# Layer 0 of a four-layer network: reciprocals of the norms spread by DMA, zeroing issued by SyncE, other mask shares, a third copy buffer, the image in eight pieces

## The chip, the cores and the metric

The kernel runs on one core of a Trainium2 chip. The metric is device time in microseconds (us): the median of several runs. One execution was also taken with the hardware profiler. Its *span* is the time from the first to the last recorded instruction; what lies around the span belongs to the run's time but not to the profile.

## What is computed

The reference is a network of four layers on one image of 256 channels and 64x64 positions. Only layer 0 is touched by the change:

```
x  = x + layer0(group_norm(x))                 # layers 1 to 3 follow
q, k = sigmoid(Wq x), sigmoid(Wk x);  v = Wv x, then divided by its norm per head and position
for w in (1, 2, 4):                            # windows of 64, 32 and 16 positions a side
    wk   = box sum of k over the window;   wkv = box sum of k v^T over the window
    attn = q . wkv ;   norm = q . wk           # per head (8 heads of 32 channels) and position
    out_w = attn / (norm + 1e-6)
layer0 = Wout [out_1, out_2, out_4] + bout
```

There is no softmax: the attention is linear, with a window as mask. Later layers contain two mixtures of experts. Their token lists `xs` (8 times 4096 rows of 256 numbers in DRAM) must be zero before rows are scattered into them; that zeroing is issued from inside layer 0.

## The kernel before, in words

**Tiles.** The 4096 positions are cut into 8 blocks of 512 (`I`, eight image rows each), and each block into 4 tiles of 128 (`J`, 8x16 positions). The 8 heads are done in two halves (`hf`) of four heads, since four heads of 32 channels fill 128 partitions. A tile name begins with `l_` in the profile where the code says `l0_`.

**Start.** `run` loads the image into `xc` with two DMAs of 2 MB, one issued by SyncE (SP) and one by ScalarE (ACT). `layer0` makes a selection matrix `sel` on GpSimd (POOL), then the window masks (`masks0`: small VectorE (DVE) operations make rows and columns, POOL multiplies them out), then `group_norm`: 16 `bn_stats` on DVE (L157) and the normalised image `y` (L162). `project0` computes q, k, v; `norms0` computes the three norms of all positions with box sums on DVE, POOL and ACT, collects them in PSUM with matmuls (L401) and takes reciprocals into `rec` (L403, L404), one row for each combination of window, block and head: 96 rows of 512.

**Main stage.** Then the pools of that stage are closed and those of the next opened: `l0o` (output weights, a zero tile), `l0w` (work) and PSUM. `half0` runs per half. POOL first builds running sums of the k v^T states of whole tiles (`F32_`, `R`, `F64_`: L415 to L424) and copies them into block-diagonal matrices `bd` (`states`, L431) when they are needed. Work then goes in *regions* (`region0`), each a list of *jobs*:

- for each half and each half image `ih`: four regions `J` for the window of 64, whose result is kept in `far["o"]`; then, for each block `I`, a region of 4 jobs that completes the window of 64 (part 0) and a region of up to 20 jobs for the windows of 32 and 16 (part 1).
- A job has a *first* part: scores of one key tile against up to four query tiles, four matmuls into the PSUM tiles `s` (L511), one tile for each pair of heads. The scores are multiplied by masks into `sm` (L529). Pair 0 is always masked by DVE, straight from PSUM. Pair 1 is first copied to SBUF by ACT (`sc`, L520, two buffers) and then masked by POOL or DVE.
- Its *second* part multiplies `sm` by v and adds into PSUM accumulators a, b, c (L553). It comes two jobs later (`self.second`).

POOL or DVE for pair 1 is decided at build time: two running sums `load0` estimate the load of both engines, with a price per mask and per tile of it, and POOL takes the mask when its sum would stay below.

**Order.** PE's (TensorE's) instructions are in the order written (`manual_schedule`). All other engines are ordered by a planner: it simulates the program with its own costs and lets each engine take the earliest written instruction that is ready. An instruction that comes late in the code but waits for nothing can thus be placed early. Each engine, SP included, then runs its list strictly in order. A tile pool has `bufs` copies per tag; a new tile waits until the last user of the old one is done.

**Output.** Results of a block go into a list `self.later`, and one entry is done after each job's first part (`out_rows`, L566). For each of three windows, `scale` spreads `rec` over the 32 channels of each head with a matmul `sel x rec` into the PSUM tile `x` and multiplies on DVE (L581). `project` then multiplies by the output weights (L137, tile `l_x_ps`, out of `l_o` and `w_out`) and adds to the image rows `xs`, which are loaded (L592) and stored to `xd` (L607) by SP.

**Zeroing.** `clear_list` is called once for each block of half 0 and has ACT issue a DMA of 4 MB that copies the zero tile over one eighth of the token lists (L1512).

Of the kernel before, what the change touches and what calls it, by code (L numbers as in the profile page):

```python
# [10 lines left out]
F32 = mybir.dt.float32  # L11
# [8 lines left out]
P = 128  # L20
# [59 lines left out]
class Net:  # L80
# [183 lines left out]
    def layer0(self, xc, x, xd, done):  # L264

        nc, tc = self.nc, self.tc
        mom = self.mom
        with tc.tile_pool(name="l0", bufs=1) as pool:
            q = [pool.tile([P, N], F32, tag=f"q{hf}", name=f"l0_q{hf}") for hf in range(2)]
            k = [pool.tile([P, N], F32, tag=f"k{hf}", name=f"l0_k{hf}") for hf in range(2)]  # L270
            v = [pool.tile([P, NT, P], F32, tag=f"v{hf}", name=f"l0_v{hf}") for hf in range(2)]
            S = [pool.tile([P, NT, D], F32, tag=f"S{hf}", name=f"l0_S{hf}") for hf in range(2)]
            rec = [pool.tile([3 * D, NB], F32, tag=f"rec{hf}", name=f"l0_rec{hf}") for hf in range(2)]
            sel = pool.tile([3 * D, NBLK, 4, D], F32, tag="sel", name="l0_sel")
            for wi in range(3):
                qs = slice(wi * D, (wi + 1) * D)
                nc.gpsimd.tensor_copy(sel[qs], bc(self.ident[qs, qs].rearrange("p (a b) -> p a b", b=4), 3, D))
            with tc.tile_pool(name="l0m", bufs=1) as tmp:
                M = self.masks0(pool, tmp)
            with tc.tile_pool(name="l0y", bufs=1) as ypool:  # L280
                self.consts0(ypool)
                y = ypool.tile([P, 2, N], F32, tag="y", name="l0_y")
                tiled = lambda a: a.rearrange("p (i j r c) -> p i r j c", i=NBLK, j=4, r=TR)
                raster = lambda a: a.rearrange("p (i r j c) -> p i r j c", i=NBLK, r=TR, j=4)
                self.group_norm(xc, lambda m: [(tiled(y[:, m])[:, i], raster(xc[:, m])[:, i]) for i in range(NBLK)])
                done()
                with (
                    tc.tile_pool(name="l0g", bufs=1) as gpool,
                    tc.tile_pool(name="l0a", bufs=2) as wp,
                    tc.tile_pool(name="l0a_ps", bufs=2, space=PSUM) as ps,  # L290
                ):
                    self.weights(ypool, ["w_qk0", "w_kv0"])
                    for hf in range(2):
                        self.project0(hf, y, q[hf], k[hf], v[hf], S[hf], wp, ps)
                        self.norms0(q[hf], k[hf], rec[hf], gpool, wp, ps)
            with (
                tc.tile_pool(name="l0o", bufs=1) as wop,
                tc.tile_pool(name="l0w", bufs=2) as wp,
                tc.tile_pool(name="l0_ps", bufs=1, space=PSUM) as ps,
            ):  # L300
                self.weights(wop, ["w_out0"])
                self.zero = wop.tile([P, C], F32, tag="zero", name="zero")
                nc.gpsimd.memset(self.zero, 0.0)
                self.load0 = [0.0, 0.0]
                bd = [[wp.tile([P, 4, P], F32, tag=f"bd{wi}{i}", name=f"l0_bd{wi}", bufs=1) for i in range(2)] for wi in range(2)]
                for b in bd[0] + bd[1]:
                    nc.gpsimd.memset(b, 0.0)
                st = [pool.tile([P, NBLK, 6], F32, tag=f"st{m}", name="l0_st") for m in range(2)]
                self.later, self.second = [], []
                with tc.manual_schedule(engines={mybir.EngineType.PE}):  # L310
                    for hf in range(2):
                        self.half0(hf, q[hf], k[hf], v[hf], S[hf], rec[hf], sel, M, bd, x, xd, st, wp, ps)
                    for go in self.second:
                        go()
                    while self.later:
                        self.later.pop(0)()
                for m in range(2):
                    nc.vector.bn_aggr(mom[:, m, :], st[m])
# [37 lines left out]

    def norms0(self, q, k, rec, ypool, wp, ps):

# [16 lines left out]
        for i in range(NBLK):  # L375
            for wi, ws in enumerate(WINS):
# [17 lines left out]
                if b > a:  # L394
# [6 lines left out]
                nc.tensor.matmul(p[wi * D : (wi + 1) * D, :], self.head_at[:, i, :], pr.rearrange("p j r c -> p (j r c)"),  # L401
                                 start=(i == 0), stop=(i == NBLK - 1))
        nc.vector.tensor_scalar_add(rec, p[: 3 * D], 1e-6)  # L403
        nc.vector.reciprocal(rec, rec)  # L404

    def half0(self, hf, q, k, v, S, rec, sel, M, bd, x, xd, st, wp, ps):
        nc, w = self.nc, self.w
        I8 = lambda a: a.rearrange("p (i j) e -> p i j e", j=4)

        F32_ = wp.tile([P, NT, D], F32, tag="F32", name="l0_F32", bufs=1)  # L410
        R = wp.tile([P, NT, D], F32, tag="R", name="l0_R", bufs=1)
        F64_ = S
# [22 lines left out]
        for ih in range(2):  # L435
# [10 lines left out]

            def rows_of(I, part, far=far, ih=ih):
                return lambda accs: self.out_rows(hf, I, accs, far["o"][:, I - 4 * ih, :], rec, sel, x, xd, st, wp, ps, part)

# [12 lines left out]
            for I in range(4 * ih, 4 * ih + 4):  # L462
                if hf == 0:
                    self.clear_list(I)

                jobs = []
                di = 4 if I < 4 else -4
# [5 lines left out]
                self.region0({"a": []}, jobs, k, v, wp, ps, rows_of(I, 0))  # L473

                b = states(1, F32_, I, slice(4 * I, 4 * I + 4))
                jobs = []
                for di in (-2, 2, -1, 0, 1):
                    if not 0 <= I + di < NBLK:
                        continue
                    for Jk in range(4):  # L480
                        j0, j1 = max(0, Jk - 1), min(3, Jk + 1)
# [12 lines left out]
    def region0(self, full, jobs, k, v, wp, ps, after):  # L494
# [12 lines left out]
        def first(i):  # L507
# [4 lines left out]
            ns = [len(range(*o[1].indices(n))) for o in outs]  # L512
            dve = sum(0.06 + 0.27 * t for t in ns)
            pool = sum(0.07 + 0.43 * t for t in ns)
            sms = []
            for pair in range(2):
                src, eng = s[pair], nc.vector
                if pair == 1:
                    src = wp.tile([P, 2, n, P], F32, tag="sc", name="l0_sc")
                    nc.scalar.copy(src, s[pair])  # L520
# [46 lines left out]

    def out_rows(self, hf, I, accs, o64, rec, sel, x, xd, st, wp, ps, part):

# [5 lines left out]

        def scale(wi, acc):
            def go():
                p = ps.tile([P, NB], F32, tag="x", name="l0_x_ps")
                ws = slice(wi * D, (wi + 1) * D)
                self.mm(p, [(sel[ws, I].rearrange("p h f -> p (h f)"), rec[ws, :])])  # L580
                nc.vector.tensor_mul(o[:, wi, :], o[:, wi, :], p)  # L581
            return go

        if part == 0:
            self.later.append(scale(0, None))
            return
# [10 lines left out]
        def project(m):  # L597
# [10 lines left out]
            return go  # L608
        self.later += [scale(1, None), scale(2, None), project(0), project(1)]

# [897 lines left out]

    def clear_list(self, k):

        part = self.xs[k * N : (k + 1) * N, :].rearrange("(p a) c -> p a c", p=P)
        self.nc.scalar.dma_start(out=part, in_=bc(self.zero, 1, N // P))  # L1512

# [410 lines left out]
    def run(self, x, out):  # L1924
        tc, nc = self.tc, self.nc
        with tc.tile_pool(name="const", bufs=1) as cpool, ExitStack() as left:
# [3 lines left out]
            for m in range(2):  # L1930
                (nc.sync, nc.scalar)[m].dma_start(out=xc[:, m, :], in_=x[m * P : (m + 1) * P, :])
            self.constants(cpool)
# [151 lines left out]
```

## Time and profile before

| | |
|---|---|
| median of 17 runs | 4570.07 us (4557.12 to 4582.64) |
| the profiled execution: its own time | 4571.75 us |
| its span | 4570.0 us |
| granted TensorE clock over the span | 0.91 |
| image, masks, group norm | 0 to 35 us |
| projections and norms of both halves | 35 to 313 us |
| main stage, half 0 | 313 to about 987 us |
| main stage, half 1 | about 987 to 1529 us |
| layers 1 to 3 | from 1530 us |
| busy over the span: PE, DVE, ACT, POOL | 83%, 40%, 26%, 33% |
| zeroing DMAs: 8 of 4096 KB | 28.3 us median from issue to landing |

How to read it: the page divides the span into 40 slices of 114 us and gives the busy share of each engine in tenths. Groups of instructions are listed by line, engine and operation, with the busy time, the mean length of one in ns, and the time that the engine sat idle just before them with the engine that ended the wait. A matmul of 32-bit numbers appears as two instructions. DMA-issuing instructions stand in the timeline with a queue's name (`SPq`, `ACTq`); their length is how long they held the engine that issues them.

### The profile page before, as it was taken

Reading aid. Unit: us, or ns where it says so; the run is one execution under the profiler, and the core shown is the slowest. Engines: PE = TensorE matmul, PEld = TensorE weight load, DVE = VectorE, ACT = ScalarE, POOL = GpSimd, SP = SyncE. Lnnn points to the kernel's source line nnn. Section 1 sums busy time; section 2 is a strip of 40 time slices with the busy share of each in tenths; the row PEclk is TensorE's granted clock in tenths of the full one; section 3 lists DMA queues with packets and bytes.
Section 4 is the critical chain, followed back from the end, with each engine's and each line's share of the span. In section 5 each row is a group of like instructions: output and inputs, shape, how many; then the busy total and the mean of one; then the engine's idle time right before and its main releaser. Section 6 shows DMA issues by size and latency. Waiting matters only on the chain.

```text
span 4570.0 us, 56172 instructions
## 1 busy us (share of the span) xinstructions
PE 3781.0 (83%) x22396; PEld 2384.7 (52%) x22396; DVE 1836.1 (40%) x3350; ACT 1180.5 (26%) x1979; POOL 1508.4 (33%) x1409
## 2 busy tenths in 40 slices
PE   6756999799999667666658877899999999799993
PEld 3311333333333356654446655566666666688882
DVE  5763565456666445545656632601111100100003
ACT  3322233233333154332112211222222212222220
POOL 3683666766666133433334300400000000000005
PEclk9867999899999888887878789999999999899996
DMA  1026000000000411110000176200000000455553
GB/s 47 0 92 214 20 19 2 19 20 10 20 10 20 141 44 56 51 44 27 0 0 29 46 225 199 64 0 10 10 10 10 10 10 10 184 194 194 194 182 118
DMA packets 149279, 291.72 MB, mean 64 GB/s; under 512 B 15248, under 2 KB 94480, under 8 KB 138768
## 3 DMA queue, kind: packets, MB, share of 16 engines
q1 hardware_dynamic: 95520, 210.01, 13.9%
q10 hardware_dynamic: 41200, 44.46, 2.9%
q0 software_dynamic: 12288, 33.57, 2.3%
q8 instruction: 178, 2.92, 0.3%
q14 instruction: 93, 0.76, 0.1%
HBM read 199.89 MB, written 88.10 MB: 63 GB/s over the span
## 4 chain that ended last, share of the span: by engine, by line
PE 43%; DVE 4%; DMA 2%; issue 2%; ACT 1%; POOL 1%; SPq 0%; POOLq 0%; DVEq 0%; ACTq 0%
PE a_o_ps L1830 10%; PE a_s_ps L137 10%; PE f_h_ps L137 8%; PE f_y_ps L137 7%; PE a_qkv_ps L137 2%; DMA f_g<-ys,f_back 1%; PE a_q_ps L137 1%; PE f_x_ps L1681 1%; DVE a_sm L1277 1%; PE a_o_ps L137 1%; PE a_u_ps L137 1%; PE a_c_ps L1302 1%; PE f_r_ps L137 0%; PE tr_ps L200 0%; DMA f_w<-in_f_w 0%
## 5 line engine op out<-in xcount | busy, mean ns | idle before, releaser
L529 POOL TENSOR_TENSOR l_sm<-l_sc,mask 128x768 f32<-128x768 f32 (+3 forms) x473 | 658.8, 1412 | 407.0 <-ACT l_sc L520 350.8
L529 DVE TENSOR_TENSOR l_sm<-l_s,mask 128x512 f32<-128x512 f32 (+3 forms) x624 | 486.5, 803 | 441.8 <-PE l_s L511 439.1
L511 PE MATMUL l_s<-l_q,l_k 32*128 32x384 f32 (+2 forms) x3584 | 493.8, 530 | 110.1 <-ACT l_sc L520 57.8
L520 ACT COPY l_sc<-l_s 128x512 f32<-128x512 f32 (+3 forms) x448 | 339.4, 758 | 841.2 <-PE l_s L511 680.3
L1830 PE MATMUL a_o_ps<-a_v,a_e 128*128 128x257 f32 x2048 | 484.3, 380 | 0.0
L137 PE MATMUL a_s_ps<-a_qT,a_kT 128*128 128x512 f32 x1024 | 482.4, 593 | 0.0
L1830 PEld LDWEIGHTS a_o_ps<-a_v,a_e 128*128 128x128 f32 x2048 | 389.1, 190 | 160.1 <-issue 118.6
L511 PEld LDWEIGHTS l_s<-l_q,l_k 32*128 32x128 f32 x3584 | 182.4, 187 | 427.4 <-DVE l_sm L529 224.1
L1724 POOL DMA_INDIRECT f_g<-ys,f_back x128 | 123.2, 962 | 811.8 <-DMA ys<-f_y 571.4
L137 PE MATMUL f_h_ps<-f_xT,f_w 128*128 128x256 f32 x1560 | 368.1, 387 | 19.0 <-ACT f_h L1693 13.4
L1593 POOL DMA_INDIRECT xs<-f_n,f_to x64 | 61.6, 963 | 921.6 <-DVE f_to L1590 643.2
L137 PE MATMUL f_y_ps<-f_w,f_h 128*128 128x256 f32 x1560 | 363.0, 380 | 2.5
L137 PEld LDWEIGHTS f_h_ps<-f_xT,f_w 128*128 128x128 f32 x1560 | 284.9, 191 | 91.1 <-ACT f_h L1693 32.5
L1825 ACT ACTIVATE a_e<-a_s_ps 128x512 f32<-128x512 f32 x256 | 152.9, 597 | 694.0 <-PE a_s_ps L137 694.0
L1693 ACT ACTIVATE f_h<-f_h_ps,f_w 128x256 f32<-128x256 f32 x390 | 184.9, 474 | 543.5 <-PE f_h_ps L137 536.9
L137 PEld LDWEIGHTS f_y_ps<-f_w,f_h 128*128 128x128 f32 x1560 | 289.0, 190 | 45.6 <-ACT f_h L1693 10.2
L818 PE MATMUL l_acc_ps<-ident,l_pr 128*128 128x128 f32 x1600 | 208.2, 290 | 121.0 <-DVE l_pr L814 116.9
L137 PEld LDWEIGHTS a_s_ps<-a_qT,a_kT 128*128 128x128 f32 x1024 | 192.3, 190 | 141.7 <-issue 129.6
L818 PEld LDWEIGHTS l_acc_ps<-ident,l_pr 128*128 128x128 f32 x1600 | 193.0, 151 | 135.9 <-DVE l_pr L814 129.2
L814 DVE TENSOR_TENSOR l_pr<-l_vk,l_w_ps 128x1280 f32<-128x1280 f32 x128 | 182.3, 1480 | 96.7 <-ACT l_w_ps L803 86.1
L1683 DVE COPY f_xT<-f_x_ps 128x512 f32<-128x512 f32 x78 | 53.9, 692 | 385.8 <-PE f_x_ps L1681 385.8
L553 PE MATMUL l_b_ps<-l_sm,l_v 128*32 128x256 f32 (+2 forms) x2176 | 176.3, 383 | 27.7 <-POOL l_sm L529 27.7
(411 smaller groups left out, 4742.8 us busy)
## 6 DMA issues: line engine op xcount, KB each, us to landing
f_w<-in_f_w SPq DMA_DIRECT2D x39, 1152.0 KB, 5.6
f_w<-in_f_w SPq DMA_DIRECT2D x39, 1028.0 KB, 7.2
xs<-zero ACTq DMA_DIRECT2D x8, 4096.0 KB, 28.3
l_vk<-vt SPq DMA_DIRECT2D x180, 128.0 KB, 2.9
f_x<-xs SPq DMA_DIRECT2D x78, 256.0 KB, 5.4
ys<-f_y SPq DMA_DIRECT2D x78, 256.0 KB, 5.3
f_w<-in_f_w SPq DMA_DIRECT2D x39, 384.0 KB, 4.0
f_w<-in_f_w SPq DMA_DIRECT2D x39, 257.0 KB, 3.5
```

What stands on the lines that cost most here:

```text
L137: self.nc.tensor.matmul(out, lhsT, rhs, start=(i == 0), stop=(i == len(pairs) - 1))
L511: nc.tensor.matmul(s[pair][:, j], k[hp, key * P : (key + 1) * P], qs[hp], start=True, stop=True)
L520: nc.scalar.copy(src, s[pair])
L529: eng.tensor_tensor(sm[:, :, at : at + t, :], src[:, :, o[1], :], bc(o[4], 1, 2), ALU.mult)
L553: nc.tensor.matmul(out, v[:, key, hp], sms[pair][:, j, base + run.start : base + run.stop], start=not seen[nm], stop=(left[nm] == 0 and ru ...
L814: nc.vector.tensor_tensor(pr, vk, bc(wps[:, j, dy], 3, D), ALU.mult)
L818: nc.tensor.matmul(acc[:, m, j, :], pf[:, dx, m * P : (m + 1) * P], self.ident, is_transpose=True, start=(j == 0 and dy == 0 and dx == 0 a ...
L1593: nc.gpsimd.indirect_dma_start(out=self.xs_parts[(b % 2) * 2 * TPB + 2 * i + r], in_=n[:, i, :], in_offset=None, out_offset=bass.IndirectO ...
L1693: nc.scalar.activation(h[:, m, :], q, AF.Gelu, bias=w1[:, 2 * hidden + m : 2 * hidden + m + 1])
L1724: nc.gpsimd.indirect_dma_start(out=y[:, :], out_offset=None, in_=self.ys[:, :], in_offset=bass.IndirectOffsetOnAxis(ap=S["back"][:, r, ti ...
L1825: nc.scalar.activation(e, p, AF.Exp, scale=1.0 / 16.0)
L1830: nc.tensor.matmul(o[i], e[:, i * P : (i + 1) * P], v[:, j, :], start=(j == 0), stop=(j == NT - 1))
```

## The change

Six things are changed, all in layer 0 or its start:

1. **Norms.** `rec` becomes a temporary tile of the pool `l0g`, stored to a DRAM tile `recd` by SP (one store per half). For each block and window, `norms` loads a tile `rcp` with SP: 4 rows of 512 from DRAM, each repeated over the 32 partitions of its head (256 KB, two buffers). `scale` becomes one DVE multiplication of two SBUF tiles. The matmul, `sel` and its three POOL copies go.
2. **Zeroing.** The zero tile is now made in `clear_list`, once for each of the 8 calls, from one buffer of the work pool, by POOL. The DMA is issued by SP.
3. **`R`** has no buffer of its own any more: it takes the one of `far["o"]` (tag `o64`).
4. **Mask shares.** The prices are 0.29 (DVE) and 0.53 (POOL) per tile of a mask, before 0.27 and 0.43.
5. **`sc`** has three buffers, before two; and the key tiles of part 1 come in the order 0, 3, 1, 2.
6. **Image.** `xc` comes in eight DMAs of 512 KB, alternating between SP and ACT.

```diff
@@ layer0
+            recd = dpool.tile([2, 3 * D, NB], F32, tag="recd", name="l0_recd")
-            rec = [pool.tile([3 * D, NB], F32, tag=f"rec{hf}", name=f"l0_rec{hf}") for hf in range(2)]
-            sel = pool.tile([3 * D, NBLK, 4, D], F32, tag="sel", name="l0_sel")
-            for wi in range(3):
-                qs = slice(wi * D, (wi + 1) * D)
-                nc.gpsimd.tensor_copy(sel[qs], bc(self.ident[qs, qs].rearrange("p (a b) -> p a b", b=4), 3, D))
...
-                self.zero = wop.tile([P, C], F32, tag="zero", name="zero")
-                nc.gpsimd.memset(self.zero, 0.0)
@@ norms0
+        rec = ypool.tile([3 * D, NB], F32, tag="rec", name="l0_rec")
         nc.vector.tensor_scalar_add(rec, p[: 3 * D], 1e-6)
         nc.vector.reciprocal(rec, rec)
+        nc.sync.dma_start(out=recd, in_=rec)
@@ half0
-        R = wp.tile([P, NT, D], F32, tag="R", name="l0_R", bufs=1)
+        R = wp.tile([P, 4, NB], F32, tag="o64", name="l0_R", bufs=1)
...
+            def norms(I, wis):
+                for wi in wis:
+                    b = wp.tile([P, NB], F32, tag="rcp", name="l0_rcp")
+                    at = wi * D + 4 * I
+                    nc.sync.dma_start(out=b, in_=bc(recd[at : at + 4, :], 1, D))
+                    rcp.setdefault(I, {})[wi] = b
...
                 if hf == 0:
-                    self.clear_list(I)
+                    self.clear_list(I, wp)
+                norms(I, (0,))
...                                              # region part 0
+                norms(I, (1, 2))
...                                              # region part 1
-                    for Jk in range(4):
+                    for Jk in (0, 3, 1, 2):
@@ region0, first
-            dve = sum(0.06 + 0.27 * t for t in ns)
-            pool = sum(0.07 + 0.43 * t for t in ns)
+            dve = sum(0.06 + 0.29 * t for t in ns)
+            pool = sum(0.07 + 0.53 * t for t in ns)
...
-                    src = wp.tile([P, 2, n, P], F32, tag="sc", name="l0_sc")
+                    src = wp.tile([P, 2, n, P], F32, tag="sc", name="l0_sc", bufs=3)
@@ out_rows
-        def scale(wi, acc):
+        def scale(wi):
             def go():
-                p = ps.tile([P, NB], F32, tag="x", name="l0_x_ps")
-                ws = slice(wi * D, (wi + 1) * D)
-                self.mm(p, [(sel[ws, I].rearrange("p h f -> p (h f)"), rec[ws, :])])
-                nc.vector.tensor_mul(o[:, wi, :], o[:, wi, :], p)
+                nc.vector.tensor_mul(o[:, wi, :], o[:, wi, :], rcp[wi])
@@ clear_list
+        zero = pool.tile([P, C], F32, tag="zero", name="zero", bufs=1)
+        self.nc.gpsimd.memset(zero, 0.0)
         part = self.xs[k * N : (k + 1) * N, :].rearrange("(p a) c -> p a c", p=P)
-        self.nc.scalar.dma_start(out=part, in_=bc(self.zero, 1, N // P))
+        self.nc.sync.dma_start(out=part, in_=bc(zero, 1, N // P))
@@ run
             for m in range(2):
-                (nc.sync, nc.scalar)[m].dma_start(out=xc[:, m, :], in_=x[m * P : (m + 1) * P, :])
+                for j in range(4):
+                    at = slice(j * N // 4, (j + 1) * N // 4)
+                    (nc.sync, nc.scalar)[j % 2].dma_start(out=xc[:, m, at], in_=x[m * P : (m + 1) * P, at])
```

More of the change, by code (lines that the diff above doesn't have):

```diff
@@ L267, in layer0 @@
         mom = self.mom
-        with tc.tile_pool(name="l0", bufs=1) as pool:
+        with tc.tile_pool(name="l0", bufs=1) as pool, tc.tile_pool(name="l0d", bufs=1, space=DRAM) as dpool:
             q = [pool.tile([P, N], F32, tag=f"q{hf}", name=f"l0_q{hf}") for hf in range(2)]
@@ L294, in layer0 @@
                         self.project0(hf, y, q[hf], k[hf], v[hf], S[hf], wp, ps)
-                        self.norms0(q[hf], k[hf], rec[hf], gpool, wp, ps)
+                        self.norms0(q[hf], k[hf], recd[hf], gpool, wp, ps)
             with (
@@ L311, in layer0 @@
                     for hf in range(2):
-                        self.half0(hf, q[hf], k[hf], v[hf], S[hf], rec[hf], sel, M, bd, x, xd, st, wp, ps)
+                        self.half0(hf, q[hf], k[hf], v[hf], S[hf], recd[hf], M, bd, x, xd, st, wp, ps)
                     for go in self.second:
@@ L355, in project0, with norms0 @@
                 (nc.scalar.copy if h % 2 else nc.vector.tensor_copy)(S[hp, ts, :], p[hp, :, hp])
-    def norms0(self, q, k, rec, ypool, wp, ps):
+    def norms0(self, q, k, recd, ypool, wp, ps):
         nc = self.nc
@@ L402, in norms0, with half0 @@
                                  start=(i == 0), stop=(i == NBLK - 1))
+        rec = ypool.tile([3 * D, NB], F32, tag="rec", name="l0_rec")
         nc.vector.tensor_scalar_add(rec, p[: 3 * D], 1e-6)
         nc.vector.reciprocal(rec, rec)
-    def half0(self, hf, q, k, v, S, rec, sel, M, bd, x, xd, st, wp, ps):
+        nc.sync.dma_start(out=recd, in_=rec)
+    def half0(self, hf, q, k, v, S, recd, M, bd, x, xd, st, wp, ps):
         nc, w = self.nc, self.w
@@ L410, in half0 @@
         F32_ = wp.tile([P, NT, D], F32, tag="F32", name="l0_F32", bufs=1)
-        R = wp.tile([P, NT, D], F32, tag="R", name="l0_R", bufs=1)
+        R = wp.tile([P, 4, NB], F32, tag="o64", name="l0_R", bufs=1)
+        R = R.rearrange("p a b -> p (a b)")[:, : NT * D].rearrange("p (t e) -> p t e", e=D)
         F64_ = S
@@ L445, in keep, with rows_of @@
                 return after
-            def rows_of(I, part, far=far, ih=ih):
-                return lambda accs: self.out_rows(hf, I, accs, far["o"][:, I - 4 * ih, :], rec, sel, x, xd, st, wp, ps, part)
+            rcp = {}
+            def norms(I, wis):
[4 more added lines that the diff above has]
+                    rcp.setdefault(I, {})[wi] = b
+            def rows_of(I, part, rcp=rcp, far=far, ih=ih):
+                return lambda accs: self.out_rows(hf, I, accs, far["o"][:, I - 4 * ih, :], rcp[I], x, xd, st, wp, ps, part)
             for J in range(4):
@@ L566, in region0, with out_rows @@
                 self.second.pop(0)()
-    def out_rows(self, hf, I, accs, o64, rec, sel, x, xd, st, wp, ps, part):
+    def out_rows(self, hf, I, accs, o64, rcp, x, xd, st, wp, ps, part):
         nc, w = self.nc, self.w
@@ L574, in out_rows @@
         o = self.o0
-        def scale(wi, acc):
+        def scale(wi):
             def go():
-                p = ps.tile([P, NB], F32, tag="x", name="l0_x_ps")
-                ws = slice(wi * D, (wi + 1) * D)
-                self.mm(p, [(sel[ws, I].rearrange("p h f -> p (h f)"), rec[ws, :])])
-                nc.vector.tensor_mul(o[:, wi, :], o[:, wi, :], p)
+                nc.vector.tensor_mul(o[:, wi, :], o[:, wi, :], rcp[wi])
             return go
         if part == 0:
-            self.later.append(scale(0, None))
+            self.later.append(scale(0))
             return
@@ L608, in project @@
             return go
-        self.later += [scale(1, None), scale(2, None), project(0), project(1)]
+        self.later += [scale(1), scale(2), project(0), project(1)]
     def bn(self, pool):
@@ L1507, in moe_consts, with clear_list @@
         nc.vector.tensor_scalar_mul(self.base, self.count[:, :NE], float(N))
-    def clear_list(self, k):
+    def clear_list(self, k, pool):
+        zero = pool.tile([P, C], F32, tag="zero", name="zero", bufs=1)
+        self.nc.gpsimd.memset(zero, 0.0)
         part = self.xs[k * N : (k + 1) * N, :].rearrange("(p a) c -> p a c", p=P)
-        self.nc.scalar.dma_start(out=part, in_=bc(self.zero, 1, N // P))
+        self.nc.sync.dma_start(out=part, in_=bc(zero, 1, N // P))
     def top2(self, pool, lg, hot, w):
```

## The prediction, made before the result was known

> **What bounds the kernel now.** I read the 40 slices first, then busy time by stretches, then the timeline around the weak stretches, then the groups by shape, and last who waits for whom.
>
> ```profile
> PE   6756999799999667666658877899999999799993
> ACT  3322233233333154332112211222222212222220
> POOL 3683666766666133433334300400000000000005
> PEclk9867999899999888887878789999999999899996
> DMA  1026000000000411110000176200000000455553
> ```
>
> Layer 0 is slices 1 to 13. From slice 5 on PE is busy at 9 tenths: the main stage is bound by PE. Its weak places are slices 3 and 4 (228 to 457 us: DMA at 2 and 6, granted clock at 6 and 7), slice 8 and, as the timeline shows, the first 35 us. The timeline of ACT in slices 3 and 4:
>
> ```profile
> 347.97 1.01 ACT L520 COPY l_sc<-l_s 128x1024 f32<-128x1024 f32 x1 [3.39 <-DVE l_sm L529]
> 347.99 11.94 ACTq L1512 DMA_DIRECT2D xs<-zero  x1
> 360.03 0.80 ACT L520 COPY l_sc<-l_s 128x768 f32<-128x768 f32 x1 [11.04 <-issue]
> 360.33 11.66 ACTq L1512 DMA_DIRECT2D xs<-zero  x1
> ...
> 385.13 11.66 ACTq L1512 DMA_DIRECT2D xs<-zero  x1
> 396.89 1.01 ACT L520 COPY l_sc<-l_s 128x1024 f32<-128x1024 f32 x1 [11.41 <-issue]
> ...
> 407.63 1.01 ACT L520 COPY l_sc<-l_s 128x1024 f32<-128x1024 f32 x1 [3.02 <-PE l_s L511]
> ...
> 414.95 1.01 ACT L520 COPY l_sc<-l_s 128x1024 f32<-128x1024 f32 x1 [1.48 <-PE l_s L511]
> ```
>
> Between two copies ACT is held for about 12 us by the issue of a zeroing DMA; PE waits for the scores' PSUM and thus for those copies. The lines at 407.63 and 414.95 are the same two jobs one region later: 7.3 us undisturbed. What gates the main stage's start:
>
> ```profile
> 312.21 0.37 SPq L115 DMA_DIRECT2D w_out<-in_w_out  x1
> 312.21 0.69 DVE L403 TENSOR_SCALAR l_rec<-l_nrm_ps 96x512 f32<-96x512 f32 x1 [2.01 <-PE l_nrm_ps L401]
> 312.24 0.31 POOL L303 MEMSET zero<- 128x256 f32 x1 [2.93 <-PE l_nrm_ps L401]
> 312.93 3.35 DVE L404 RECIPROCAL l_rec<-l_rec 96x512 f32<-96x512 f32 x1
> 339.39 2.08 PE L540 MATMUL l_a_ps<-l_q,l_bd 128*128 128x128 f32 x8 [11.06 <-POOL l_bd L431]
> ```
>
> The weights' load and POOL's first memset both start when the last matmul of the old pools ends, at 312.2, though the normalised image whose place they take was read long before: the new pools wait for the whole of the old ones. From there POOL's sums take 27 us and PE waits for them. The part that the first edit removes:
>
> ```profile
> L137 PE MATMUL l_x_ps<-l_rec,l_sel 32*128 32x512 f32 x96 | 49.0, 589 | 0.9 <-DVE l_o L581 0.9
> L581 DVE TENSOR_TENSOR l_o<-l_o,l_x_ps 128x512 f32<-128x512 f32 x48 | 32.7, 681 | 3.1 <-PE l_x_ps L137 3.1
> ```
>
> **The change, part by part.** Times are against the profiled execution, 4571.75 us (span 4570.0), which lies 1.7 above the median of 4570.07; the sum is then taken from the median.
>
> *Image in eight pieces, `sel` gone: -8.* Before, DVE's first `bn_stats` starts at 14.25, when 2 MB have landed, and DVE then needs until 30.67, with 15.2 us busy and two waits of 1.5 and 1.1 for POOL. The 4 MB come over about 12 us, so the first two pieces (1 MB) should land near 5. DVE's 16.4 us counted from there end at 21.6; the first matmul (35.18, 1.27 after l_y starts) and the weights' load (30.19, when POOL's masks end) follow the same DVE operations. That is at most 9, less where DVE's list waits for a later piece: 4 to 12, the upper end if masks fill the gaps, since 16 statistics at 0.61 after the last pieces could end sooner. POOL's three copies (3 x 1.03) sat under that load. The six more issues at 0.4 are split over two idle queues; `pp` behind them on SP is first read after 300 us.
>
> *Zeroing off ACT: -42.* At 343.6 POOL's states are there and PE restarts; the score matmuls of the fourth job end at 345.8, so its copy could stand at 345.8, and the next region's first copy 7.3 later at 353.1, not at 396.89: 43.8. PE's clock is 0.60 of full between 313 and 363, so I take 2 off: 42, with 30 to 44 as ends. SP gets 8 issues of 0.7 to 12.9 us. Behind them in its list stand the `rcp` loads and one image load; its next job in the trace is the store at 502.51, after a gap from 312.69, and 8 x 12 = 96 us fit in that. If that cover went, the first blocks would wait.
>
> The Trainium skill (DMA: Bandwidth & Descriptors, Issuing engines are not separate DMA queues) speaks against this term: all issuers share 16 engines, and another issuer saves only the issuing time, usually small beside the transfer. By that rule the edit would be worth about nothing; this trace has issues of 11.4 us median under landings of 28.3, so I go by the row.
>
> *`rec` must be stored before the pools close: +6.6.* If the whole old pools gate the new, the start at 312.2 moves behind L403 (0.69), L404 (3.35) and a store. The nearest store is `xd`'s, 2.7 from issue to landing. 0.7 + 3.3 + 2.6 = 6.6 on POOL's chain, which PE waits for. Ends: 0, if only the place of `rec` is gated, and 7.3.
>
> *Zero tile of one buffer: +8.* Each of the seven later memsets (0.31 on POOL) now waits for the DMA before it; POOL runs in order, so masks and states behind it wait too, and PE for them. 4 MB at the 350 GB/s of the stretch 313 to 413 are 12.0, with 2.7 to land about 14.7 a round. The trace has no such wait. Nothing is lost if the planner places a memset after the real landing; if it is 1 us early each time, 7 us, and 15 if 2 us. I take 8, as its costs look short for loads (it put four `bn_stats` ahead of mask operations that were ready at 6 us, and the load landed at 14).
>
> *No matmul for `scale`: -34.* 48 pairs hold PE for 0.95 each (790.54 to 791.49). For windows 32 and 16 the next scores could not have started at once: masks and copy of the job before end 0.70 before the actual start (791.78 against 792.48; 789.1 against 789.78). For window 64 the eight bd matmuls follow and cover it. 16 x (0.95 + 0.70 + 0.68) = 37; a little off for the waits that become longer: 34; ends 24 (0.5 each) and 46.
>
> *The same multiplication from two SBUF tiles: +4.* From PSUM it takes 681 ns. Masks of the same size from SBUF take 748 on DVE on average, but one took 1.67 us beside POOL. 48 x 0.07 = 3 to 48 x 0.98 = 47 of DVE time; DVE is 63% busy here and holds PE for part of that: 0 to 15.
>
> *48 loads of `rcp`: 0.* 256 KB each, two buffers. The tight one is window 64's: its buffer comes free with window 32's multiplication of the block before (789), it is needed at 803, and 256 KB loads land in 5.4 (`f_x`). Cover 14 us; if SP stands behind the store of `xd` (801.3) instead, see the rivals. The trace shows no load of this pattern; ends 0 and 5 per block, 80 in all, of which I take 0 since loads come 13 us ahead.
>
> The Trainium skill (same page, Rules for kernel authors) says that a transfer whose outermost dimension is below 16 uses only that many DMA engines; here the source has 4. With its 27 GiB/s an engine and 2 us fixed it would be an estimated 4.3 us, which changes nothing under 14.
>
> *Mask shares, third `sc` buffer, key order: -6.* Working the two prices through all jobs in their order gives 473 pair-1 masks for POOL and 151 for DVE before, as the trace counts them, and 467 and 157 after. Wide ones move: with the mean lengths by width (POOL 0.67 to 2.13, DVE 0.46 to 1.29) POOL loses 50 us busy and DVE gains 27. Outside 800 to 840, PE waits after 460 for POOL masks add to 14 us; ACT's waits for POOL, which the third buffer shortens, to 98 over the stage. I take half of 14; one off for DVE. Ends: -14 and +5 (DVE late next). The key order only pairs the same widths differently: 0.
>
> *`R` shares with `far`: -6.* In block 5 of half 0 POOL builds the sums for half 1 in one piece (806 to 833), and the block takes 81.1 us from store to store against 58.1 for the same block of half 1. Now only `F32_` (5.7) may run there; `R` and `F64_` (13, with bd 15.6) wait for the last use of `far` in block 7, some 25 us ahead of need. Two smaller holes for one: 23 lost before, about 17 after. Ends -15 and +10.
>
> *Tail: -3.* The last two `scale` steps on PE (1516.36 to 1520.30) shrink to DVE's two multiplications: -2 to -5.
>
> Sum: -8 - 42 + 6.6 + 8 - 34 + 4 - 6 - 6 - 3 = -80.4; 4570.07 - 80.4 = 4489.7, say **4490 us** (-1.8%). Layers 1 to 3 are shifted as a whole.
>
> **The rivals.**
>
> *A, slower: the zero memsets stand early in POOL's list.* Then the DMA's rounds hold the states instead of ACT. For it: POOL's states are a chain with gaps, and the planner did put small copies between them (320.75, 322.86). Against: it must think 4 MB land in a few us. All seven rounds ahead of the states: 7 x 14.7 = 103 in place of the 8 above, hence 4585; it decides at six rounds or more.
>
> *B: loads of `rcp` come late.* SP keeps w64's load behind the store of the same block's rows; landing 5 us after need, 14 times, of which PE feels 4: +56, 4546. Against it: the buffer is free 12 us before.
>
> *C: the zeroing's cost only moves.* Rounds spread over half 0 hold POOL for 2 to 6 us each: the -42 is eaten, about 4532.
>
> *D: more is won*: no gate at 312 and no memset waits: 4475 or less.
>
> **How the numbers follow.** The forecast 0.67, A 0.10, B 0.06, C 0.10, D 0.07. The terms' half-ranges (4, 7, 4, 8, 10, 8, 9, 12) add as squares to 23, so the forecast's own range is 4467 to 4520; D and C stretch it to 4460 and 4548. A lies outside, with some of B and D: 0.18. A measurement here can tell about 0.2%, 9 us. Slower is A without its mildest forms, and what I have not seen: 0.10; same 0.03; faster 0.87.
>
> **What would show it.** Right: ACT's queue has no zeroing, the copy that stood at 396.89 stands near 353 (8 for the earlier start, 42 less 6.6 here), no PE matmul out of `sel`, the main stage starts about 6.6 us after the last norm matmul, block 5 of half 0 is near 62. Wrong: POOL's memset of `zero` ends long idle times; DVE waits for `rcp`; a hole of over 15 us at the change of halves, where `R` comes late.

## The result, and the profile after

The changed kernel takes 4596.28 us (median of 8 runs, 4591.60 to 4602.40) against 4568.26 for the kernel before (median of 47 runs, 4557.12 to 4582.64). The ratio is 1.0063, with an interval of 1.0053 to 1.0074: 0.63% or some 29 us slower, where 1.8% faster was forecast. The profiled execution of the changed kernel took 4589.27 us, with a span of 4587.6 and a granted clock of 0.907. It lies 7 us under its median, so the two profiles show 17.5 of the difference.

The 40 slices of the changed kernel, the same five rows that were shown of the kernel before:

```profile
PE   6747888878998767666658878799999999799993
ACT  3312223223232153342112211222221122222220
POOL 3684556666565233433323300400000000000005
PEclk9968999989999888887878789999999999899995
DMA  1017100000001421111000166200000000455553
```

The zeroing has moved together (DMA 1 and 7 in slices 3 and 4, before 2 and 6), and slice 4 is busier on PE (7, before 6). But slices 5 to 8, where PE stood at 9 tenths three times out of four, now read 8 throughout. So the start got better and the main stage behind it worse. Landmarks from the two timelines give the size, in us from the start of the span:

| | before | after | difference |
|---|---|---|---|
| first matmul of the projections | 35.2 | 28.7 | -6.5 |
| end of the last norm matmul | 312.2 | 305.5 | -6.7 |
| first matmul with the states `bd` | 339.4 | 342.9 | +3.5 |
| eighth copy of scores (the one at 396.89) | 396.9 | 356.2 | -40.7 |
| sum of window 64, block 0 | 460.0 | 444.8 | -15.2 |
| last store of layer 0 | 1529.1 | 1550.0 | +20.9 |
| end of the program | 4570.0 | 4587.6 | +17.5 |

There are three losses: 10.2 us between the second and the third row, 25.5 between the fourth and the fifth, 36.1 between the fifth and the sixth. The first two can be read in the timeline of the changed kernel (start, length, engine, line, operation; in brackets the idle time before it and what ended that):

```profile
306.23 3.35 DVE L399 RECIPROCAL l_rec<-l_rec 96x512 f32<-96x512 f32 x1
...
309.60 0.32 SPq L400 DMA_DIRECT2D l_recd<-l_rec  x1
...
311.80 1.92 POOL L301 MEMSET l_bd<- 128x512 f32 x4 [9.19 <-DMA l_recd<-l_rec]
...
356.17 1.01 ACT L529 COPY l_sc<-l_s 128x1024 f32<-128x1024 f32 x1 [1.43 <-PE l_s L520]
...
362.08 0.31 POOL L1518 MEMSET zero<- 128x256 f32 x1 [6.59 <-DMA xs<-zero]
362.35 2.12 POOL L538 TENSOR_TENSOR l_sm<-l_sc,mask 128x1024 f32<-128x1024 f32 x1
...
421.17 0.31 POOL L1518 MEMSET zero<- 128x256 f32 x1 [11.17 <-DMA xs<-zero]
421.42 0.28 POOL L428 COPY l_bd<-l_S 32x128 f32<-32x128 f32 x1
```

The new pools open at 311.8, when the store of `rec` has landed, 6.3 us after the last norm matmul (305.5). This wait is called the gate below. The other 3.9 of the first loss are about what two masks of 2.12 take that now stand among POOL's sums for `bd` (at 314.67 and 335.26, none before). The copy stands at 356.17 with PE's scores as its only wait. And POOL stands idle in front of the memsets of `zero`, up to 11.17 us, with masks and states queued behind them.

The third loss is in the groups by shape, in 305 to 1552 us (busy time, mean ns | idle before and its releasers):

```profile
L587 DVE TENSOR_TENSOR l_o<-l_o,l_rcp 128x512 f32<-128x512 f32 x48 | 71.7, 1517 | 8.1 <-ACT l_o L593 7.4 <-ACT l_o L594 0.4
```

Before, the same 48 multiplications, with one operand from PSUM, took 681 ns each. Now their mean is 1517. Taken singly in the trace, 27 of the 48 last over 1 us, all of them for windows 32 and 16; in 12 of the 16 blocks both are long. Who waits for that, in the same stretch (total, times, longest), after:

```profile
PE l_s L520 <- DVE l_sm L538: 95.7, 114, 3.8
POOL zero L1518 <- DMA xs<-zero: 43.9, 6, 11.2
```

and before, in 313 to 1525 us:

```profile
PE l_s L511 <- DVE l_sm L529: 49.1, 93, 2.3
```

PE's wait for DVE's masks has grown by 46.6 us, and its longest from 2.3 to 3.8. One such place, from the timeline of the changed kernel:

```profile
472.27 4.17 POOL L538 TENSOR_TENSOR l_sm<-l_sc,mask 128x1024 f32<-128x1024 f32 x2 [2.59 <-ACT l_sc L529]
...
472.71 4.28 DVE L587 TENSOR_TENSOR l_o<-l_o,l_rcp 128x512 f32<-128x512 f32 x2 [0.43 <-ACT l_o L593]
...
476.92 0.94 DVE L538 TENSOR_TENSOR l_sm<-l_s,mask 128x768 f32<-128x768 f32 x1
...
477.92 1.40 PE L520 MATMUL l_s<-l_q,l_k 32*128 32x384 f32 x8 [3.65 <-DVE l_sm L538]
```

At the end of a block ACT copies windows 32 and 16 into `o`, and at that moment POOL gets its two masks of the next part. DVE's two multiplications start 0.4 us after POOL's first mask and take 4.28 us together. DVE's own mask waits behind them, and PE for the mask. Taken singly, the trace shows an alternation: POOL's first mask ends at 474.40 and the first multiplication at 474.95; POOL's second mask, 768 wide, runs from 474.36 to 476.44, 2.08 us where 1.65 is usual, and the second multiplication ends at 476.99. Each multiplication ends 0.55 us after the POOL mask that it ran beside.

### The profile page after: what moved, and what is told of

It reads as the page before. It is cut to its first block, busy times and chain, and to the rows that moved or that the text cites. A ratio compares the mean times of both kernels' runs of the same rounds, so it can differ in the third digit from the quotient of the medians.

```text
span 4587.6 us, 54886 instructions
## 1 busy us (share of the span) xinstructions
PE 3763.8 (82%) x21788; PEld 2358.8 (51%) x21788; DVE 1888.9 (41%) x3356; ACT 1179.9 (26%) x1979; POOL 1465.5 (32%) x1407
## 3 DMA queue, kind: packets, MB, share of 16 engines
q1 hardware_dynamic: 135408, 256.54, 16.9%
## 4 chain that ended last, share of the span: by engine, by line
PE 43%; DVE 4%; issue 2%; DMA 2%; ACT 1%; POOL 1%; SPq 0%; ACTq 0%; DVEq 0%; POOLq 0%
PE a_o_ps L1838 10%; PE a_s_ps L137 10%; PE f_h_ps L137 8%; PE f_y_ps L137 7%; PE a_qkv_ps L137 2%; PE a_q_ps L137 1%; DMA f_g<-ys,f_back 1%; PE f_x_ps L1689 1%; PE a_o_ps L137 1%; DVE a_sm L1283 1%; PE a_u_ps L137 1%; PE a_c_ps L1308 1%; DMA f_w<-in_f_w 1%; PE tr_ps L200 1%; PE f_r_ps L137 0%
## 5 line engine op out<-in xcount | busy, mean ns | idle before, releaser
L538 POOL TENSOR_TENSOR l_sm<-l_sc,mask 128x512 f32<-128x512 f32 (+3 forms) x467 | 614.6, 1333 | 427.5 <-ACT l_sc L529 426.2
L520 PE MATMUL l_s<-l_q,l_k 32*128 32x384 f32 (+2 forms) x3584 | 499.2, 541 | 122.5 <-DVE l_sm L538 95.7
L137 PEld LDWEIGHTS f_y_ps<-f_w,f_h 128*128 128x128 f32 x1560 | 289.0, 190 | 45.6 <-ACT f_h L1701 10.2
```

The costliest lines, as they stand in the source:

```text
L137: self.nc.tensor.matmul(out, lhsT, rhs, start=(i == 0), stop=(i == len(pairs) - 1))
L520: nc.tensor.matmul(s[pair][:, j], k[hp, key * P : (key + 1) * P], qs[hp], start=True, stop=True)
L538: eng.tensor_tensor(sm[:, :, at : at + t, :], src[:, :, o[1], :], bc(o[4], 1, 2), ALU.mult)
```

## The experiments

The changes in microseconds below are differences of the ratios to the kernel before, times 4568.

**The theory.** Two of the new costs were priced far too low: the multiplication of two SBUF tiles beside POOL's masks (DVE late, PE behind it), and the memsets of the one-buffer zero tile. **The rivals:** the rest of the norms part (loads of `rcp`, gate of the pools) costs the time; ACT's two copies come too late and it is not the operand; the new prices load DVE too much; the copies' third buffer or `R` in the buffer of `far` costs more than it saves.

### One zero tile again

```diff
@@ layer0
+                self.zero = wop.tile([P, C], F32, tag="zero", name="zero")
+                nc.gpsimd.memset(self.zero, 0.0)
@@ clear_list
-        zero = pool.tile([P, C], F32, tag="zero", name="zero", bufs=1)
-        self.nc.gpsimd.memset(zero, 0.0)
...
-        self.nc.sync.dma_start(out=part, in_=bc(zero, 1, N // P))
+        self.nc.sync.dma_start(out=part, in_=bc(self.zero, 1, N // P))
```

> The changed kernel with one zero tile, made once in the pool of the output weights as before; SP still issues the eight DMAs. Theory Z (the memsets of the one-buffer zero tile wait for the DMA before them: POOL idles 43.9 us for it, and from the first region to the first block's end 25 us are lost): those waits go, the first block's window-64 multiplication (445.6 in the changed kernel) comes near 420, and the time falls by 20 to 30 us, to about 4571. Rival (the zeroing costs wherever it stands, now as SP issues of 11 us each with the loads of the reciprocals behind them): no gain, 4590 to 4600.

Measured: 4570.41 us, ratio 1.0008 (0.9998 to 1.0017), so 25 us better than the changed kernel. From the first `bd` matmul to the sum of window 64 it takes 71.6 us (348.3 to 419.9), in the changed kernel 102.0: the memsets cost 30 us there, not 8. The `bd` matmul itself comes 5.4 later, because the gate grew. The fourth experiment, which has the same edit, shows why in its timeline:

```profile
304.82 0.67 SPq L1519 DMA_DIRECT2D xs<-zero  x1
...
308.48 7.30 SPq L402 DMA_DIRECT2D l_recd<-l_rec  x1
...
321.24 1.93 POOL L303 MEMSET l_bd<- 128x512 f32 x4 [16.52 <-DMA l_recd<-l_rec]
```

The one zero tile is filled by 304.7, right after PE's last norm matmul (304.3), so the first zeroing DMA no longer waits for the pools that the store holds up. It is issued ahead of the store of `rec`, whose own issue now takes 7.30 us, and the pools open 16.9 us after the last norm matmul.

### The multiplication from PSUM

Windows 32 and 16 are multiplied straight out of their PSUM accumulators; window 64 stays as it is in the changed kernel.

```diff
-                nc.vector.tensor_mul(o[:, wi, :], o[:, wi, :], rcp[wi])
+                src = o[:, 0, :] if wi == 0 else accs["abc"[wi]]
+                nc.vector.tensor_mul(o[:, wi, :], src, rcp[wi])
...
-        nc.scalar.copy(o[:, 1, :], accs["b"])
-        nc.scalar.copy(o[:, 2, :], accs["c"])
```

> The changed kernel, but windows 32 and 16 are multiplied straight out of their PSUM accumulators, so DVE reads one operand from SBUF and not two, and ACT's two copies a block go. Theory P (a DVE multiplication of two SBUF tiles that starts beside a POOL instruction ends 0.55 us after it: 2.1 to 2.2 us in place of 0.69, masks and PE wait behind): the 32 multiplications take 0.69, PE's wait for DVE's masks (95.7) falls to about 50, and the time falls by 40 to 65 us, to 4530 to 4556. Rival S (the new prices, the key order and the third buffer are what slows the blocks): multiplications get short, but the blocks of half 1 stay near 62 us, and the gain is at most 10 us.

Measured: 4523.82 us, ratio 0.9907 (0.9891 to 0.9924): 71 us better than the changed kernel, more than the 40 to 65 expected. The same place in its timeline:

```profile
470.53 0.68 DVE L588 TENSOR_TENSOR l_o<-l_b_ps,l_rcp 128x512 f32<-128x512 f32 x1
470.59 3.74 POOL L538 TENSOR_TENSOR l_sm<-l_sc,mask 128x1024 f32<-128x1024 f32 x2 [2.59 <-ACT l_sc L529]
...
471.12 0.68 DVE L588 TENSOR_TENSOR l_o<-l_c_ps,l_rcp 128x512 f32<-128x512 f32 x1
...
471.72 0.95 DVE L538 TENSOR_TENSOR l_sm<-l_s,mask 128x768 f32<-128x768 f32 x1
...
472.73 0.93 PE L520 MATMUL l_s<-l_q,l_k 32*128 32x384 f32 x8
```

POOL's masks run at the same moment, and the multiplications take 0.68 each. PE's wait for DVE's masks is back where it was before the change:

```profile
PE l_s L520 <- DVE l_sm L538: 49.9, 101, 1.3
```

The stretch from the sum of window 64 to the end of layer 0 shows that it is more than the wait. By stretches of time (length, then busy time and number of PE, PEld, DVE, ACT and POOL, granted clock, DMA share, GB/s), after:

```profile
445.00:1550.00 1105.00, 960.26 (x8460) 348.18 (x8456) 683.32 (x849) 333.55 (x458) 645.93 (x564) 0.95 0.09 28
```

and with the operand from PSUM:

```profile
443.00:1479.00 1036.00, 935.89 (x8464) 342.05 (x8456) 642.88 (x851) 317.62 (x426) 640.85 (x564) 0.98 0.09 29
```

It is 69 us shorter. 24 of that is PE busy time, with the same matmuls (four records aside), at a granted clock of 0.98 instead of 0.95; the other 45 is idle time of PE, about what the wait for DVE's masks lost (95.7 - 49.9 = 45.8). DVE itself is only 40 us less busy. That the stalls lower the clock is the reading that fits: in the profiles of the three kernels that multiply two SBUF tiles (the changed one, the one with one zero tile, and the norms alone) the stretch from the sum of window 64 to the end of layer 0 has a clock of 0.95, in the other eleven 0.97 to 0.98. No run here sets it apart.

### ACT's copies kept as idle work

The multiplication from PSUM as above, but the two `nc.scalar.copy` stay (their result is overwritten).

> The changed kernel with the multiplications of windows 32 and 16 out of PSUM as in the second run, but ACT's two copies a block stay as dead work (the multiplication overwrites their result). Theory P (DVE's second SBUF operand makes it wait for POOL): within 10 us of the second run, 4514 to 4534. Rival (that run gained because ACT lost 32 copies of 0.59 and the multiplication no longer stands behind them): most of the 72 us is gone again, 4570 to 4596.

Measured: 4534.05 us, ratio 0.9921 (0.9904 to 0.9937), 65 us better than the changed kernel. At the same place POOL's mask starts at 471.77, and DVE stands just as it did in the changed kernel, 0.45 after that start and behind ACT's copy:

```profile
472.22 0.69 DVE L588 TENSOR_TENSOR l_o<-l_b_ps,l_rcp 128x512 f32<-128x512 f32 x1 [0.43 <-ACT l_o L594]
```

It takes 0.69 us where the changed kernel takes 2.24. So it is the place of the operand, not the copies. The 6 us between this run and the second are no more than their overlapping intervals allow without any effect.

### The norms as before, all else changed

`rec` in two tiles, `sel` and its matmul again; no store, no `rcp`, no gate.

```diff
-                nc.vector.tensor_mul(o[:, wi, :], o[:, wi, :], rcp[wi])
+                p = ps.tile([P, NB], F32, tag="x", name="l0_x_ps")
+                self.mm(p, [(self.sel[ws, I].rearrange("p h f -> p (h f)"), rcp[wi])])
+                nc.vector.tensor_mul(o[:, wi, :], o[:, wi, :], p)
```

> The changed kernel with its first part undone: reciprocals stay in SBUF and are spread by the matmul out of sel; the other five parts stay. Theory P: blocks come back to the times before (58.1 for block 5 of half 1, now 62.1) and the 6.3 us gate at the main stage's start goes: 4536 to 4556. Rival S: only the gate goes and the matmuls come back: 4590 to 4625.

Measured: 4540.56 us, ratio 0.9939 (0.9922 to 0.9955). The norms part as it was written thus costs 57 us on top of the rest of the change. With the operand from PSUM it gains: the second experiment is 15 us faster than this one and the one with the copies kept 8, though both pay the gate of 6.3. Without the gate the missing matmul is worth some 14 to 21 us, the upper figure with ACT's copies gone too. About 1 us of it is the making of `sel`: the last norm matmul ends at 304.8 here and at 303.8 in the second experiment.

### The norms alone

The kernel before with `rec` stored, `rcp` loaded and the multiplication from two SBUF tiles; image, zeroing, shares, buffers and key order as before.

> The kernel before with the first part of the change alone: reciprocals through DRAM, multiplication of two SBUF tiles, no matmul, no sel. Theory P: with wide POOL masks at the same place, the part costs by itself what undoing it gave in the third run (56 us), less the 6 us of the gate, which the zeroing on ACT hides: 40 to 55 slower than before, 4608 to 4623. The prediction's terms for it (-34 + 4): 4538. Rival S: as the prediction, since prices and buffers are the old ones.

Measured: 4614.90 us, ratio 1.0101 (1.0083 to 1.0120), 46 us slower than the kernel before; in the profiles 8.7 us lie ahead of the first `bd` matmul (348.1, before 339.4). The group by shape (309 to 1573 us):

```profile
L588 DVE TENSOR_TENSOR l_o<-l_o,l_rcp 128x512 f32<-128x512 f32 x48 | 76.6, 1622 | 7.5 <-ACT l_o L594 7.2
```

Here 32 of the 48 take over 1 us, and PE's wait for DVE's masks is 110.8 us. The cause is in this part of the change alone and needs none of the other parts, the new prices among them.

### The zeroing alone on SP

```diff
-        self.nc.scalar.dma_start(out=part, in_=bc(self.zero, 1, N // P))
+        self.nc.sync.dma_start(out=part, in_=bc(self.zero, 1, N // P))
```

> The kernel before with one word changed: SP issues the eight zeroing DMAs in place of ACT, from the one zero tile. The prediction's term: -42, so 4524 (30 to 44 off, 4522 to 4536). Rival C of the prediction (the cost only moves, to the loads behind them): 4555 to 4566. As the reciprocals stay in SBUF, nothing that the main stage's start needs stands behind the zeroing.

Measured: 4517.44 us, ratio 0.9893 (0.9875 to 0.9911): one word is worth 49 us, the largest gain of all parts and above the 30 to 44 that the prediction allowed. The issues are no shorter on SP (duration min/median/max in ns):

```profile
L1512 SPq DMA_DIRECT2D xs<-zero x8: 672/11180/12852, 311.6 to 383.6; - x8
```

They land 28.5 us after issue, 28.3 before. Only the engine that is held has changed. The Trainium skill (DMA: Bandwidth & Descriptors, Issuing engines are not separate DMA queues) is right that another issuer makes no transfer faster; that the issuing time is usually small beside it did not hold for these 4 MB issues of 11 us.

### Both repairs, and `rec` where nothing waits for it

The fourth run has one zero tile and the multiplication from PSUM. The sixth adds to it that `rec` lies in the pool of the whole layer:

```diff
+            self.rpool = pool
...
-        rec = ypool.tile([3 * D, NB], F32, tag="rec", name="l0_rec")
+        rec = self.rpool.tile([3 * D, NB], F32, tag="rec", name="l0_rec")
```

> The changed kernel with one zero tile made once and with the multiplications of windows 32 and 16 out of PSUM. If theories Z and P are right and add, 60 to 95 us less than the changed kernel: about 4516, which would be faster than the kernel before by 1%. If both rivals are right: 4585 to 4600.

> The fourth run's kernel (one zero tile, multiplications out of PSUM) with the reciprocals' tile moved from the pool that is closed before the main stage to the layer's own pool; it is still stored and loaded by DMA. Theory G (the main stage's work pool opens only when the store has landed, 16.5 us after POOL is free in the fourth run, because the store stands behind the first zeroing DMA on SP): the first bd matmul, 43.7 us after the last norm matmul in the fourth run, comes after about 28, and the time falls by 13 to 17 us, to 4483 to 4487. Rival (the opening waits for something else, such as the memory of the norms' sums): within 3 us of the fourth run's 4500.

Measured: 4499.89 us (0.9854, 0.9837 to 0.9870) and 4485.64 us (0.9827, 0.9809 to 0.9845). The first gains 95 us on the changed kernel, and 71 + 25 = 96: the two costs add. The second opens the pools at once:

```profile
304.68 1.93 POOL L304 MEMSET l_bd<- 128x512 f32 x4
```

Its first `bd` matmul comes at 331.1 instead of 348.0, but its last store only 19 us earlier, and the medians differ by 12 to 14.

### Shares, third buffer, `R`

The eighth run is the sixth with the old prices and the old key order; the eleventh the sixth with two `sc` buffers; the twelfth the eleventh with `R` in a buffer of its own.

```diff
@@ eighth run
-                    for Jk in (0, 3, 1, 2):
+                    for Jk in range(4):
...
-            dve = sum(0.06 + 0.29 * t for t in ns)
-            pool = sum(0.07 + 0.53 * t for t in ns)
+            dve = sum(0.06 + 0.27 * t for t in ns)
+            pool = sum(0.07 + 0.43 * t for t in ns)
@@ eleventh and twelfth run
-                    src = wp.tile([P, 2, n, P], F32, tag="sc", name="l0_sc", bufs=3)
+                    src = wp.tile([P, 2, n, P], F32, tag="sc", name="l0_sc")
@@ twelfth run
-        R = wp.tile([P, 4, NB], F32, tag="o64", name="l0_R", bufs=1)
-        R = R.rearrange("p a b -> p (a b)")[:, : NT * D].rearrange("p (t e) -> p t e", e=D)
+        R = wp.tile([P, NT, D], F32, tag="R", name="l0_R", bufs=1)
```

> The sixth run's kernel with the old prices (0.27 and 0.43) and the old key order; three buffers stay. If prices and order help as the prediction's term has it: 2 to 6 us slower than the sixth run. Rival S (they hurt): 5 us or more faster. Nothing: within 2 us.

> The sixth run's kernel with two sc buffers in place of three. ACT's waits for POOL's release of sc were 98 us in the kernel before and 13 in the changed one after its first 100 us; if they reached PE, 5 to 14 us slower than the sixth run (4491 to 4500); if PE's waits are set by POOL's masks themselves: within 3 us of it.

> The eleventh run's kernel with R in a buffer of its own, as before. The prediction's term: sharing saves 6 us, so this one is 6 slower than the eleventh. Rival: the two builds of the sums cost the same or more than the one in block 5 (block 5 of half 0: 69.5 us shared against 81.1; block 7: 63.1 against 46.9): 5 us faster or more.

Measured, in this order: 4480.67 us (0.9807, 0.9791 to 0.9824), 4487.83 (0.9828, 0.9809 to 0.9848) and 4498.97 (0.9854, 0.9834 to 0.9874). Old shares and order are 5 us lower than new ones by the medians, 9 by the ratios, with overlapping intervals: no gain of the new ones can be seen, and perhaps a small loss. Prices and order were not set apart, so a gain of one may hide a loss of the other. The order does more than pair widths: the window of 16 takes 1,472 matmul records (`l_c_ps`) in the new order and 1,984 in the old, but PE is busy with them for 144 us in both. A gain of the third buffer can't be seen (2 us by the medians). `R` in the buffer of `far` is worth 11 us: the intervals of the ratios, which carry the spread of the kernel before as well, overlap a little, but the runs themselves don't (4483.66 to 4492.36 against 4495.11 to 4504.94). Its blocks 5 and 7 of half 0, by stretches of time, with `R` shared:

```profile
744.60:808.90 64.30, 55.48 (x505) 20.70 (x504) 36.77 (x51) 17.48 (x24) 43.21 (x36) 0.95 0.09 30
863.20:921.40 58.20, 44.45 (x352) 15.66 (x348) 28.14 (x36) 12.58 (x16) 44.34 (x44) 0.85 0.10 32
```

and with `R` of its own:

```profile
746.40:826.20 79.80, 60.10 (x504) 20.95 (x504) 36.83 (x51) 17.48 (x24) 58.33 (x52) 0.83 0.07 24
880.60:927.25 46.65, 41.87 (x348) 15.40 (x348) 28.14 (x36) 12.58 (x16) 29.32 (x28) 0.93 0.12 40
```

15 us of POOL's sums have moved from block 5 to block 7 (fifth busy figure); block 5 is 15.5 shorter and block 7 11.6 longer, and 4 remain. Of the other 7, 2 arise ahead of block 5 and 5 in half 1; what makes those isn't shown.

The eighth run is the fastest of all: 1.9% under the kernel before, about 2.5% under the changed one.

### The image alone in eight pieces

The kernel before with the new loop of loads, `sel` still made.

> The kernel before with the image in eight pieces, sel's copies on POOL kept. The changed kernel's first matmul came 6.5 us earlier: 4 to 7 us off, 4561 to 4564; if the masks wait for sel's copies (3 us on POOL): 3 to 4 off.

Measured: 4554.06 us, ratio 0.9970 (0.9959 to 0.9980), so 14 us, where 4 to 7 were expected. The first matmul of the projections starts at 32.1 (before 35.2), but the last norm matmul ends at 303.2 (before 312.2): of these 9.0 us 5.9 arise after that first matmul, which the prediction had not looked at. What makes them, and the rest of the 14, isn't shown.

## Why the prediction was wrong

**The step that failed is "the same multiplication from two SBUF tiles: +4".** Its size is +65 to +71: the place of the operand alone gives that back in two experiments (65 with ACT's copies kept, 71 without them), and the norms part alone makes the kernel 46 us slower where its terms (-34, +4, +6.6 and -3) add to -26. The prediction had the row: a mask from SBUF of 1.67 us beside POOL (of the 68 masks of that size that DVE made from SBUF the longest even took 2.13). It went wrong in two choices. First, it took the upper end (47 us of DVE time) as unlikely, though the list sets these multiplications exactly where POOL gets its widest masks: at a block's end, behind ACT's copies. The kernel before showed as much: its multiplication of window 32 at 490.13 ran while POOL masked from 488.21 to 491.95. Second, it took only a part of DVE's time to be PE's, because "DVE is 63% busy and holds PE for part of that". A share of busy time says nothing on that: the late mask is the next thing PE needs, and in 15 of the 16 blocks at least one multiplication was long. 40 us of DVE time became 45 of PE's idle time and 24 of slower matmuls. The Trainium skill (SBUF — State Buffer, Who interferes with whom) states the case: a DVE instruction with two inputs in SBUF contends with a GpSimd instruction that reads SBUF, over a shared pair of ports that one locks for a whole instruction. The trace agrees: the multiplications end 0.55 us after POOL's mask, POOL's second mask is held 0.43, and from PSUM nothing is held.

**"Zero tile of one buffer: +8" is 30.** The direction and the mechanism were right: memsets wait for the DMA before them (43.9 us of POOL's idle time, in six waits), and masks and states stand behind. The step took the planner to place each memset 1 to 2 us early; it places them up to 11.2 us early. The sign the prediction named, long idle times ended by POOL's memset of `zero`, is in the trace. Rival A, which had the memsets ahead of the states, isn't what happened (the first waiting one comes at 362, after the first states); that its 4585 lies nearest to the 4596 is chance. Rival C comes nearest in its mechanism: 25.5 of the 40.7 us won by moving the zeroing were lost again by the sum of window 64.

**"No matmul for `scale`: -34" is 14 to 21,** below its lower end of 24. The sum took the matmul's 0.95 and the waits of 0.70 and 0.68 behind it as lost almost in full, once in each block. Which of them still passes without the matmul isn't shown.

Right in direction and mechanism were these. *Zeroing off ACT* (-42): 49 alone, above its upper end of 44, and the copy that was to stand near 353 stands at 356.17. *Gate of `rec`* (+6.6): 6.3. *Loads of `rcp`* (0): no wait of DVE for them is in the trace, so rival B has no trace of itself; when these loads land isn't recorded, so the prediction's estimate of 4.3 us for one stays untested. *Image* (-8): 14, outside its upper end of 12 though; the reading that DVE is busy for 15.2 us there is wrong (13.8 between 14.25 and 30.67), but no term rests on it. *`R` with `far`* (-6): 11, in the range; block 5 takes 69.5 us in the changed kernel, not the 62 named. *Shares, buffer, order* (-6): nothing measurable, in the range; no run speaks against the 0 for the key order, though the order does more than pair widths. The *tail* (-3) was not measured. And the half-ranges, which add to 23, give 4467 to 4513, not to 4520.

With the measured sizes the sum reads -14 - 49 + 6 + 30 - 14 + 65 + 0 - 11 = +13, or +18 to +22 with the 5 to 9 us of the shares, against +29 measured. The same sum for the sixth run, which has none of the three costs, is -14 - 49 - 21 - 11 = -95, against -79 measured: it misses by as much, so the remainder doesn't lie in those costs. The parts were measured beside different companions; which of them is dearer in company stays open. Without the three wrong or avoidable costs (+4, +8, +6.6) the prediction's own sum gives 4471; the kernel without them took 4485.64. That the forecast of 4490 lies near this is partly luck: image, zeroing and `R` brought 18 us more than priced, the missing matmul 13 to 20 less.

## What to carry to other kernels

Before an operand of a DVE instruction is moved from PSUM to SBUF, see in the timeline what POOL does at that moment: here a DVE multiplication of two SBUF tiles that started beside a POOL mask ended only after that mask, and as PE's next work stood behind it on DVE, PE waited too. A one-buffer tile that is refilled for each of a row of DMAs made the filling engine wait for six landings, with all that was queued behind it; a constant is made once. Price such terms at the place in the list where they stand, not by the share of busy time of their engine.

## What the runs showed of the hardware

- A 128x512 multiplication on DVE with both inputs in SBUF took 0.67 to 0.69 us with POOL idle and 2.1 to 2.2 beside a POOL mask of 2.08 to 2.13; it ended 0.55 after it. POOL's masks of 768 took 2.08 instead of 1.65 where a multiplication got in between. From PSUM: 0.68 to 0.69 beside the same masks.
- Eight 4 MB DMAs from a small tile, issued one after another, held SP for 0.67 to 12.9 us each, 11.2 in the median (the zeroing alone on SP); issued each after the landing of the one before, as in the changed kernel, 0.53 to 0.64. A 192 KB store issued behind one had an issue of 7.30 us instead of 0.32, and the pools opened 16.9 us after the last norm matmul instead of 6.3.
- Stalls of PE of up to 3.8 us at the blocks' ends went with a granted clock of 0.95 over the main stage; with the operand in PSUM it was 0.98, and the same matmuls (8,460 records) took 936 us instead of 960. That the stalls are the cause isn't shown.
